# First batch group of a two-layer graph kernel: two columns of products become four tasks in two bank sets

## The chip, the cores and the metric

The kernel runs on one core of a Trainium2 chip. The metric is the device time of one execution in microseconds (us), lower is better. Three runs of the kernel before took 2121.89, 2118.05 and 2122.76 us; the median is 2121.89 us. A difference of about 0.2% (4.2 us) is what a measurement of this kernel can tell from no change.

## The reference

128 batches, each with 128 nodes and 512 features, go through two layers. All data is float32.

```python
# layer 0
deg = jnp.sum(adj, axis=-1, keepdims=True)
agg = jnp.einsum('bij,bjf->bif', adj, x) / jnp.maximum(deg, EPS)
cat = jnp.concatenate([x, agg], axis=2)
x   = _layernorm(x + jax.nn.relu(jnp.einsum('bnf,of->bno', cat, W)))
# layer 1
Xw = X @ Wv + bv
sj = Xw @ aw[:d, 0]
si = Xw @ aw[d:, 0]
e = leaky_relu(sj[:, None, :] + si[:, :, None] + ab[0], negative_slope=0.2)
alpha_matrix = A * jnp.exp(e)
transition = alpha_matrix / (jnp.sum(alpha_matrix, axis=-1, keepdims=True) + 1e-12)
for k in range(3):
    H = H + Xk @ Wk[k] + bk[k]
    Xk = jnp.einsum('bij,bjd->bid', transition, Xk)
x = _layernorm(x + relu(H))
```

Only two parts of it matter for this change. The first is the product of x with the two halves of W, for the first four batches. The second is the folding of constants: the kernel never forms Xw, but folds Wv and aw into two extra weight columns, and bv, ab and bk into constants that layer 1 uses.

## The kernel before

The 128 batches are worked in 32 groups of four. Layer 0 runs over all groups first, then layer 1. Within a group, x is split into an upper pair of batches (`xu`) and a lower pair (`xl`), and every large product is a fast block product with seven multiplications in place of eight (the constants `LEFT` and `RIGHT` name the seven left and right operands). The left operands need four sums of quarter blocks of x (`left_sums`, called by `x_inner`), after x has been loaded in blocks (`load_left`) and transposed on VectorE (`x_turn`). The right operands need four sums of quarter blocks of the weights (`w_inner(0)` for the two weight blocks of output column 0, `w_inner(1)` for those of column 1).

From the second group on, the scheme of seven is used a second time, over the blocks of batches and weights: the tasks `P12`, `P56`, `P74` and `T` of a group. It needs further sums, `w_outer(1)` to `w_outer(4)`, of 1792 columns each, two of them on VectorE and two on GpSimd. The first group can't wait for these sums, so the function `first` computes it with the inner scheme only. It computes output column 0 and then column 1, each as seven products, and each product covers both pairs of batches: four matmuls of 256 columns, `xu` into the left half of a PSUM bank and `xl` into the right half. Four banks (`bA`) hold the running sums, called X, Y, W and Z. The results of column 0 go to SBUF, to be multiplied by the normalized adjacency; those of column 1 are copied into the other four banks (`bB`), onto which `first_last` then accumulates that product.

A float32 matmul shows in the trace as two passes. A product of `first` therefore shows as eight passes, four on `xu` and four on `xl`.

The order of the work on each engine is written out by hand. `steps` is a list of pieces of tasks (one `yield` is one piece, mostly one product). Work beside the products is placed by a number: position 2t is just after piece t's own instructions, and 2t + 1 is after the pending evictions (`late`). `START` holds these positions for the beginning of the kernel. Inside an engine instructions keep this order, so an instruction that waits holds up all that stand behind it. Ahead of the list stand the first loads, which are put on two queues (SyncE's, shown as SP, and ScalarE's, shown as ACT), and the first transposes and sums. The load DMAs share eight completion semaphores in turn, so at most eight of them are on their way at a time.

`fold_constants` is a generator of seven pieces. It loads nothing itself; its matmuls use `bk_sb`, `aw_sb` and `wvt_sb`, and at its end it fills two banks once with zero-padded copies of the identity, to leave them in a defined state. In the kernel before its pieces stand between the products of the first group, and its matmuls use banks of `bB`.

Of the kernel before, what the change touches and what calls it, by code (L numbers as in the profile page):

```python
# [16 lines left out]
def kernel(  # L17
# [92 lines left out]
    wvt_sb = [p2.tile([P, 2, F], FP, name=f"wvt{i}", tag="y") for i in range(2)]  # L110
# [3 lines left out]
    bk_sb = p1.tile([K, F], FP, name="bk_sb", tag="TT")  # L114
# [5 lines left out]
    load_w0([nc.scalar], 1)  # L120
    load_w0([nc.scalar], 3)
    load_adj(0)
    for i in range(2):
        nc.sync.dma_start(wvt_sb[i], wvt[i * FH : (i + 1) * FH, :].rearrange("(c p) f -> p c f", p=P))
# [32 lines left out]
    def fold_constants():  # L157
        ones_row = ones[:].to_broadcast([P, P])
        pb, pc, pw = bB[0], bB[3], bB[0]
        nc.tensor.matmul(pb, ones_row[:K], bk_sb, start=True, stop=True)  # L160
        L_.copy(beta[:, 0, 254:], pb[:, :131])
        L_.copy(beta[:, 1, :381], pb[:, 131:])
        t4 = small.tile([P, NC], FP, name="t4")
        V.tensor_add(t4, aw_sb[:, 0], aw_sb[:, 1])
        V.tensor_mul(t4, t4, bv_sb)
        t1 = small.tile([P, 1], FP, name="t1")
        V.tensor_reduce(t1, t4, AX.X, ALU.add)
        yield
        nc.tensor.matmul(pc[:, :1], ones_row, t1, start=True, stop=True)
        V.tensor_sub(beta[:, 1], beta[:, 1], beta[:, 0])  # L170
        V.tensor_add(cc, pc[:, :1], ab_sb)
        yield
        for c in range(NC):
            nc.tensor.matmul(pw[:2], aw_sb[:, :, c], wvt_sb[c // 2][:, c % 2, :], start=(c == 0), stop=(c == NC - 1))
            if c % 2:
                yield
        w2row = p1.tile([2, NC, Q, R], FP, name="w2row", tag="TT")
        L_.copy(w2row, pw[:2].rearrange("t (q c s) -> t c q s", q=Q, c=NC))
        yield
        for c in range(NC):  # L180
            mm(pc[:, 2 * c : 2 * c + 2], w2row[:, c].rearrange("t q s -> t (q s)"), ident[:2, :2], c == 0)
        L_.copy(stage[:, :, 3 * F : 3 * F + 2], pc[:, : 2 * NC].rearrange("p (c t) -> p c t", c=NC))
        for t in (pw, pc):
            nc.tensor.matmul(t, ident, ident[:, None, :].to_broadcast([P, Q, P]), start=True, stop=True)
        yield
# [71 lines left out]
    def x_inner(n, p):  # L257
        need(("x_turn", n, p, 1))
        t = (xu, xl)[p][n]
        left_sums([S_, S_, S_, S_], [t[:, :, i] for i in range(7)])  # L260
# [71 lines left out]
    def p12(lane, g):  # L332
        r, c11 = rs[g], c11s[g] = blocks(p2, "r"), blocks(p2, "c11")
# [15 lines left out]
    def p74(lane, g):  # L349
        r, c22, c21 = rs[g], blocks(p2, "c22"), blocks(p2, "c21")  # L350
# [76 lines left out]
    def first(lane, g):  # L427
        c11, c21 = blocks(p2, "c11"), blocks(p2, "c21")
        c11s[g], c21s[g] = c11, c21

        def column(o, bank_of, evict):
            X, Y, W, Z = [bA[i] for i in bank_of]

            def prod(dst, k, start=False):
                for h in range(2):
                    for i in range(2):
                        mm(dst[:, h * FH : (h + 1) * FH], (xu, xl)[h][g][:, i, LEFT[k]], wf[:, SLOT[2 * i + o], RIGHT[k]],
                           start and i == h == 0)
            s5 = halves()
            prod(X, 1, True)  # L440
            L_.copy(Y, X)
            yield
            prod(Z, 5, True)
            L_.copy(s5, Z)
            yield
            prod(X, 6)
            V.tensor_add(W, X, s5)
            yield
            prod(Y, 2)
            yield  # L450
            prod(X, 7)
            evict(BY, Y)
            V.tensor_add(Z, X, s5)
            yield
            prod(W, 3)
            yield
            prod(X, 4)
            evict(BWW, W)
            evict(BZ, Z)
            late.append((evict, BX, X))  # L460
            yield

        def evict0(b, t):
            L_.copy(part(c11, b), t[:, :FH])
            V.tensor_copy(part(c21, b), t[:, FH:])
        yield from column(0, (0, 1, 2, 3), evict0)

        def evict1(b, t):
            i, h = b
            L_.copy(bB[i][:, h * FH : (h + 1) * FH], t[:, :FH])  # L470
            V.tensor_copy(bB[2 + i][:, h * FH : (h + 1) * FH], t[:, FH:])
        yield from column(1, (1, 2, 0, 3), evict1)
        lane[:] = [bA[2], bA[3], bA[1], bA[0]]

    def first_last(lane, g):
        new_mv(g)
        for p, t in ((1, c21s[g]), (0, c11s[g])):
            for i in range(2):
                b = 2 * p + i
                mm(bB[b], aTs[g][:, b], t[:, i, :, :FH])  # L480
                late.append((residual, g, b, bB[b]))
            yield
        lane[:] = [bB[2], bB[0], bB[1], bB[3]]
# [274 lines left out]
    TASKS = {"F": first, "FL": first_last, "P12": p12, "P56": p56, "P74": p74, "T": last, "O1": o1, "O2": o2, "O5": o5,  # L758
             "O6": o6, "O7": o7, "O4": o4, "O3": o3, "C": combine}
    lanes = [list(bA), list(bB)]  # L760
# [4 lines left out]

    PA = "p74.5 P12.1 P12.2 p74.6 P12.3 p74.7 P12.4 t.1 P12.5 P12.6 t.2 P12.7 P56.1 t.3 P56.2 t.4 t.5 P56.3 t.6 t.7 t.8 t.9 t.10 t.11 P74.1 P74.2 P56.4 P56.5 P56.6 P74.3 P56.7 P74.4".split()
# [7 lines left out]
    for k in range(14):  # L774
        step(0, "F", 0, k + 1)
# [84 lines left out]
    def fold(i):  # L860
        next(folding, None)
# [9 lines left out]
    def w_outer(i):  # L871
        need(("w_inner", 1), *{1: [], 2: [("w_outer", 1)], 3: [("F", 0, 14)], 4: [("w_outer", 2)]}[i])
# [4 lines left out]
        ("w_inner", 1): 9, ("x_s2", 1): 30, ("fold", 2): 3, ("a_turn", 0): 16, ("w_outer", 2): 16, ("fold", 4): 11,  # L877
        ("degree", 0): 10, ("a_norm", 0): 10, ("load_left", 1, 1): 9, ("x_s1", 1): 21, ("fold", 5): 16, ("fold", 3): 8,
        ("w_outer", 1): 11, ("fold", 7): 10, ("fold", 6): 17, ("x_s3", 1): 22, ("w_outer", 4): 19, ("load_y", 0, 0): 17,
        ("load_y", 0, 1): 9, ("x_turn", 1, 0, 0): 14, ("a_load", 0): 15, ("x_turn", 1, 0, 1): 14, ("x_inner", 1, 0): 16,  # L880
        ("x_turn", 1, 1, 1): 18, ("load_left", 1, 0): 12, ("x_turn", 1, 1, 0): 10, ("fold", 1): 4, ("x_inner", 1, 1): 19,
        ("w_outer", 3): 33, ("load_left", 2, 1): 19, ("load_adj", 1): 26, ("load_left", 2, 0): 23, ("load_wk",): 58,
    }
    OPS.update({f.__name__: f for f in (w_inner, w_outer, fold, load_wk)})
# [21 lines left out]
    for p in range(2):  # L906
        run([(x_turn, 0, p, 0), (x_turn, 0, p, 1)])
    run([(x_inner, 0, 0), (x_inner, 0, 1), (w_inner, 0)])
    gens, count, held_by = {}, {}, {}
    ET = mybir.EngineType  # L910
    with tc.manual_schedule(engines={ET.PE, ET.DVE, ET.Activation, ET.Pool, ET.SP}):
        for t, (lane, name, g, k) in enumerate(steps):
            if name:
                if (name, g) not in gens:
                    if lane in held_by:
                        need((*held_by[lane], {"F": 14, "FL": 2, "T": 11, "C": 8}.get(held_by[lane][0], 7)))
                    held_by[lane] = name, g
                    gens[name, g] = TASKS[name](lanes[lane], g)
# [33 lines left out]
```

## Time and profile before

| quantity | value |
|---|---|
| median of three runs | 2121.89 us (2118.05 to 2122.76) |
| the profiled execution's own time | 2123.95 us |
| its span, first to last instruction | 2122.2 us |
| TensorE busy | 2088.1 us, 98% of the span |
| VectorE, ScalarE, GpSimd busy | 69%, 54%, 73% of the span |
| first product of the first group starts | 11.06 us |
| first product of the second group starts | 51.32 us |

The profiled execution takes 1.75 us more than its span, and 2.06 us more than the median of the three runs. Times inside it are counted from the start of the span. A row of the timeline gives the start, the duration, the engine, the source line, the operation and its tiles, and the number of instructions that were merged into it; a note in square brackets tells how long the engine was idle before and what ended that. A row of a table of windows gives, for each stretch of time, the busy time of every engine with its number of instructions, the mean clock that TensorE was granted (1.00 is full speed), the share of the DMA engines that was in use, and what they moved.

### The profile page before, as it was taken

To read this page: it belongs to the slowest core of one execution; us is meant where nothing else is said; L and a number is where in the kernel's file an instruction comes from. 1 tells how busy PE (TensorE), PEld (TensorE's weight loads), DVE (VectorE), ACT (ScalarE), POOL (GpSimd) and SP (SyncE) were. 2 spreads that over 40 slices of the span, in tenths; PEclk is the share of its full clock that TensorE was granted. 3 is DMA by queue.
4 is the path that set the end of the run, shared out by engine and by line. 5 is a ranking of instruction groups with operands and counts; after the bars stand their busy time and mean duration, and the time that the engine had idled before them with its cause. 6 is when DMAs were issued, how large, how long until landed. Compare 5 with 4: busy or idle time off the path is not lost. (4 is left out here: it accounts for less than half of the span.)

```text
span 2122.2 us, 25957 instructions
## 1 busy us (share of the span) xinstructions
PE 2088.1 (98%) x7104; PEld 1329.5 (63%) x7104; DVE 1462.4 (69%) x3229; ACT 1149.4 (54%) x2885; POOL 1539.5 (73%) x1427
## 2 busy tenths in 40 slices
PE   8999999999999999999999999999999999999996
PEld 5887888888788886555555555555555555555552
DVE  4777777777777776666666666666666666666654
ACT  2665666666566665354454454554554554554554
POOL 4877888887777775767767777777677677677662
PEclk9999999999999999999999999999999999999998
DMA  7766666566666668235335335335335345344332
GB/s 170 181 192 188 188 185 175 159 187 193 162 174 181 181 170 236 68 96 131 92 101 130 89 100 137 82 100 139 80 102 134 84 106 132 82 111 128 83 86 95
DMA packets 429454, 287.13 MB, mean 135 GB/s; under 512 B 153465, under 2 KB 352249, under 8 KB 429308
## 3 DMA queue, kind: packets, MB, share of 16 engines
q1 hardware_dynamic: 428060, 283.62, 50.0%
q10 hardware_dynamic: 1120, 1.84, 0.4%
q8 instruction: 56, 0.92, 0.2%
q14 instruction: 90, 0.74, 0.1%
q0 software_dynamic: 128, 0.01, 0.0%
HBM read 191.60 MB, written 93.79 MB: 134 GB/s over the span
## 5 line engine op out<-in xcount | busy, mean ns | idle before, releaser
L149 PE MATMUL bA<-big,xu 128*128 128x256 f32 (+1 forms) x1834 | 579.9, 436 | 3.3 <-DVE r L611 1.0
L149 PEld LDWEIGHTS bA<-big,xu 128*128 128x128 f32 x1834 | 346.3, 190 | 178.5 <-issue 27.3
L149 PE MATMUL bB<-big,xl 128*128 128x256 f32 (+1 forms) x1330 | 398.9, 416 | 0.3 <-ACT bB L565 0.2
L149 PE MATMUL bA<-big,xs 128*128 128x256 f32 (+1 forms) x1316 | 387.9, 418 | 0.4 <-ACT bA L565 0.2
L149 PEld LDWEIGHTS bB<-big,xl 128*128 128x128 f32 x1330 | 251.7, 189 | 99.9 <-issue 14.8
L149 PEld LDWEIGHTS bA<-big,xs 128*128 128x128 f32 x1316 | 244.8, 189 | 93.0 <-DVE bA L574 14.6
L149 PE MATMUL bB<-big,xu 128*128 128x256 f32 (+1 forms) x868 | 286.5, 441 | 2.5 <-DVE bB L388 2.5
L149 PE MATMUL bB<-c,TT 128*128 128x512 f32 x512 | 247.6, 596 | 0.0
L608 POOL TENSOR_TENSOR s<-s,r 128x385 f32<-128x385 f32 x128 | 127.9, 1000 | 153.3 <-DVE bA L574 108.4
L493 ACT ACTIVATE junk<-y,mv 128x512 bf16<-128x512 f32 x256 | 184.5, 721 | 80.2 <-POOL mv L488 76.1
L149 PEld LDWEIGHTS bB<-big,xu 128*128 128x128 f32 x868 | 159.0, 189 | 91.8 <-DVE r L598 19.2
L506 ACT ACTIVATE y<-y,mv,rstd 128x512 f32<-128x512 f32 x256 | 204.1, 811 | 3.1 <-POOL mv L501 3.1
L149 PE MATMUL bA<-big,xl 128*128 128x385 f32 (+1 forms) x490 | 182.1, 478 | 4.6 <-DVE xl L254 4.5
L574 DVE TENSOR_TENSOR bA<-bA,s 128x385 f32<-128x385 f32 x128 | 72.5, 567 | 164.5 <-ACT s L571 117.8
L371 DVE SCALAR_TENSOR_TENSOR y<-bB,y 128x512 f32<-128x512 f32 x256 | 170.6, 683 | 19.8 <-PE bB L149 13.6
L149 PE MATMUL bB<-big,xs 128*128 128x385 f32 x448 | 173.4, 492 | 0.9 <-POOL xl L242 0.9
L149 PEld LDWEIGHTS bB<-c,TT 128*128 128x128 f32 x512 | 97.6, 191 | 90.4 <-issue 48.7
L745 ACT COPY bB<-r 128x512 f32<-128x512 f32 x64 | 37.7, 590 | 191.0 <-DVE big L744 189.3
L277 POOL TENSOR_TENSOR xu<-xu,xs 128x896 f32<-128x896 f32 x63 | 131.4, 2086 | 10.1 <-PE bA L149 10.1
L149 PEld LDWEIGHTS bA<-big,xl 128*128 128x128 f32 x490 | 93.8, 192 | 71.6 <-DVE c L611 7.9
L273 POOL TENSOR_TENSOR xl<-xu,xl 128x896 f32<-128x896 f32 x63 | 133.4, 2117 | 1.1
L269 POOL TENSOR_TENSOR xs<-xs,xu 128x896 f32<-128x896 f32 x63 | 131.8, 2092 | 2.4
(160 smaller groups left out, 3537.0 us busy)
## 6 DMA issues: line engine op xcount, KB each, us to landing
xb<-in_x_dram SPq DMA_DIRECT2D x256, 128.0 KB, 3.5
y<-in_x_dram SPq DMA_DIRECT2D x64, 512.0 KB, 4.4
yd<-y SPq DMA_DIRECT2D x64, 512.0 KB, 2.8
xb<-yd SPq DMA_DIRECT2D x256, 128.0 KB, 3.8
y<-yd SPq DMA_DIRECT2D x64, 512.0 KB, 4.3
out_dram<-y SPq DMA_DIRECT2D x64, 512.0 KB, 2.8
ag<-in_adj_dram SPq DMA_DIRECT2D x64, 256.0 KB, 3.9
sb<-sd SPq DMA_DIRECT2D x252, 64.0 KB, 3.2
```

The costliest lines, as they stand in the source:

```text
L149: nc.tensor.matmul(dst, lhsT, rhs, start=start, stop=True, skip_group_check=True)
L269: S_.tensor_sub(xs[n][:, 1], xs[n][:, 0], xu[n][:, 0])
L273: S_.tensor_sub(xl[n][:, 0], xu[n][:, 0], xl[n][:, 0])
L277: S_.tensor_sub(xu[n][:, 1], xu[n][:, 1], xs[n][:, 1])
L371: V.scalar_tensor_tensor(y, t, 0.0, y, ALU.max, ALU.add, accum_out=mvs[n][:, b, 0:1])
L493: L_.activation(junk, ys[n, b // 2][:, b % 2], AF.Square, bias=mvs[n][:, b, 0:1], accum_out=mvs[n][:, b, 1:2])
L506: L_.activation(y, y, AF.Identity, bias=mvs[n][:, b, 0:1], scale=rstds[n][:, b : b + 1])
L574: V.tensor_add(W, X, s5)
L608: S_.tensor_add(s5, s5, part(src, BZ, BW))
L745: L_.copy(at_[b], row(b, 254, 766, 1))
```

## The change

The change touches only the first group and what stands beside it and the second group.

1. `first` becomes four tasks: A is column 0 with the upper pair, B column 0 with the lower pair, C column 1 with the upper pair, D column 1 with the lower pair. Each has seven products of two matmuls. A and B share the banks `bA`, C and D the banks `bB`; A and C use the left halves of the banks, B and D the right halves. The list `PF` gives the order of the 28 pieces. Column 1 is now evicted into `bA`, and `first_last` and the second group's lanes have the bank sets exchanged.
2. The fold's seven pieces move from beside the first group to beside the second (after `first_last`), on two banks of `bA`. The load of `wvt` moves with them, to a place behind the store of the normalized adjacency.
3. Of the loads of weight blocks 1 and 3, half go from ScalarE's queue to SyncE's. SyncE's queue has the x blocks of the second group in another order, and the two loads of y (x in row order, for the residual) earlier.
4. The left sums of the first group go from GpSimd to VectorE; those of the lower pair, and its transposes, stand between the products of A and B. `w_outer(2)` and `w_outer(4)` stand ahead of the second group's left sums on GpSimd.

```diff
-    wvt_sb = [p2.tile([P, 2, F], FP, name=f"wvt{i}", tag="y") for i in range(2)]
+    wvt_sb = [p2.tile([P, 2, F], FP, name=f"wvt{i}", tag="c22") for i in range(2)]
...
     load_left(0, 1)
-    load_w0([nc.scalar], 1)
-    load_w0([nc.scalar], 3)
+    load_w0([nc.scalar, nc.sync], 1)
+    load_w0([nc.scalar, nc.sync], 3)
     load_adj(0)
-    for i in range(2):
-        nc.sync.dma_start(wvt_sb[i], wvt[i * FH : (i + 1) * FH, :].rearrange("(c p) f -> p c f", p=P))
+
+    def load_wvt():
+        for i in range(2):
+            nc.sync.dma_start(wvt_sb[i], wvt[i * FH : (i + 1) * FH, :].rearrange("(c p) f -> p c f", p=P))
...
     def fold_constants():
-        pb, pc, pw = bB[0], bB[3], bB[0]
+        need(("FL", 0, 2))
+        pb, pc, pw = bA[2], bA[3], bA[2]
...
-        left_sums([S_, S_, S_, S_], [t[:, :, i] for i in range(7)])
+        left_sums([S_ if n else V] * 4, [t[:, :, i] for i in range(7)])
...
+    def first(g, o, h):
+        X, Y, W, Z = [t[:, h * FH : (h + 1) * FH] for t in (bA, bB)[o]]
+        if o == 0:
+            dst = blocks(p2, "c21" if h else "c11")
+            (c21s if h else c11s)[g] = dst
+        else:
+            need(("w_inner", 1))
+
+        def prod(dst, k, start=False):
+            for i in range(2):
+                mm(dst, (xu, xl)[h][g][:, i, LEFT[k]], wf[:, SLOT[2 * i + o], RIGHT[k]], start and i == h == 0)
+
+        def evict(b, t):
+            if o == 0:
+                to = part(dst, b)
+            else:
+                need(("FA", 0, 7), ("FB", 0, 7))
+                to = bA[2 * h + b[0]][:, b[1] * FH : (b[1] + 1) * FH]
+            if (b[0] + b[1]) % 2:
+                L_.copy(to, t)
+            else:
+                V.tensor_copy(to, t)
+        s5 = halves()[:, :FH]
+        if h:
+            need(("F" + "AC"[o], 0, 2))
+        prod(X, 1, True)
+        L_.copy(Y, X)
+        yield
+        prod(Z, 5, True)
+        L_.copy(s5, Z)
+        yield
+        prod(X, 6)
+        V.tensor_add(W, X, s5)
+        yield
+        prod(Y, 2)
+        late.append((evict, BY, Y))
+        yield
+        prod(X, 7)
+        V.tensor_add(Z, X, s5)
+        yield
+        prod(W, 3)
+        late.append((evict, BWW, W))
+        yield
+        prod(X, 4)
+        late.append((evict, BZ, Z))
+        late.append((evict, BX, X))
+        yield
...
-    lanes = [list(bA), list(bB)]
+    lanes = [[bB[1], bB[3], bB[0], bB[2]], list(bA)]
...
+    PF = "A.1 A.2 A.3 A.4 A.5 A.6 B.1 B.2 B.3 C.1 B.4 A.7 C.2 B.5 C.3 B.6 B.7 C.4 C.5 C.6 D.1 D.2 D.3 D.4 D.5 D.6 C.7 D.7".split()
...
     START = {
...
+        ("fold", 2): 81, ("x_inner", 0, 1): 13, ("load_y", 0, 0): 7, ("fold", 5): 86, ("fold", 4): 85, ("degree", 0): 23,
+        ("load_left", 2, 1): 59, ("x_s3", 1): 50, ("w_outer", 3): 64, ("load_left", 2, 0): 36, ("x_turn", 1, 1, 0): 37,
+        ("x_turn", 1, 0, 1): 39, ("load_left", 1, 1): 17, ("load_y", 0, 1): 13, ("w_inner", 1): 16, ("load_wk",): 74,
+        ("fold", 3): 81, ("x_s2", 1): 54, ("a_norm", 0): 25, ("x_turn", 1, 0, 0): 30, ("fold", 6): 91, ("x_s1", 1): 48,
+        ("w_outer", 1): 22, ("w_outer", 2): 34, ("w_outer", 4): 37, ("load_wvt",): 32, ("fold", 7): 102,
+        ("x_inner", 1, 0): 44, ("a_load", 0): 35, ("x_turn", 0, 1, 1): 8, ("a_turn", 0): 59, ("x_turn", 1, 1, 1): 37,
+        ("load_left", 1, 0): 4, ("fold", 1): 77, ("x_inner", 1, 1): 38, ("load_adj", 1): 47, ("x_turn", 0, 1, 0): 6,
     }
...
-    for p in range(2):
-        run([(x_turn, 0, p, 0), (x_turn, 0, p, 1)])
-    run([(x_inner, 0, 0), (x_inner, 0, 1), (w_inner, 0)])
+    run([(x_turn, 0, 0, 0), (x_turn, 0, 0, 1), (x_inner, 0, 0), (w_inner, 0)])
```

## The prediction

> **What bounds the kernel now.** I read the page first, then the granted clock and busy time by stage, then the timeline of the first stages, then the waits of the start.
>
> ```profile
> PE 2088.1 (98%) x7104; PEld 1329.5 (63%) x7104; DVE 1462.4 (69%) x3229; ACT 1149.4 (54%) x2885; POOL 1539.5 (73%) x1427
> ...
> PE   8999999999999999999999999999999999999996
> ...
> PEclk9999999999999999999999999999999999999998
> ```
>
> TensorE is busy 98% of the span, and the slices show it full everywhere but in the first and last of 40. So the change can win only where TensorE isn't full, or runs slowly: at the start, which is all it touches.
>
> ```profile
> core 0: us, PE busy (x) PEld busy (x) DVE busy (x) ACT busy (x) POOL busy (x), PEclk, DMA share, GB/s
> 2.65:11.06 8.41, 8.41 (x16) 3.75 (x17) 1.73 (x5) 0.00 (x0) 3.05 (x8) 1.00 1.15 214
> 11.06:16.61 5.55, 1.03 (x5) 0.57 (x4) 4.55 (x7) 0.48 (x1) 2.55 (x3) 0.93 1.15 214
> 16.61:23.37 6.76, 6.76 (x14) 4.37 (x15) 0.54 (x1) 1.96 (x3) 2.85 (x4) 0.55 1.10 276
> 23.37:51.32 27.95, 27.95 (x119) 20.56 (x119) 14.10 (x25) 7.59 (x25) 13.82 (x11) 1.00 0.52 131
> 51.32:76.20 24.88, 24.88 (x107) 19.96 (x106) 19.59 (x40) 15.21 (x39) 21.56 (x19) 1.00 0.85 193
> ```
>
> The first stage is warming up on the identity. In the second TensorE has 1.03 us of work in 5.55. In the third it is busy, but at a granted clock of 0.55. The fourth is the rest of the first group, the fifth the second group with nothing missing: what a stage costs when it is fed.
>
> ```profile
> 11.06 1.03 PE L149 MATMUL bA<-big,xu 128*128 128x256 f32 x4
> ...
> 15.84 1.30 DVE L254 STREAM_TRANSPOSE xl<-xb 128x512 f32<-128x512 f32 x2 [1.00 <-issue]
> 16.13 1.28 ACT L441 ACT_TABLE_LOAD   x1 [16.13 <-DMA big<-in_w0t_dram]
> ...
> 16.61 2.07 PE L149 MATMUL bA<-big,xl 128*128 128x256 f32 x4 [4.52 <-DVE xl L254]
> ...
> 18.48 1.91 PE L149 MATMUL bA<-big,xu 128*128 128x256 f32 x4
> ...
> 24.34 1.03 PE L149 MATMUL bA<-big,xl 128*128 128x256 f32 x4
> ```
>
> ```profile
> PE bA L149 <- DVE xl L254: 4.5, 1, 4.5
> ```
>
> The first product does its four passes on `xu` at 11.06 us and stops: its four on `xl` need the transposes at 15.84, and those the last quarter of `xb`. TensorE stands from 11.93 to 16.61. Then four passes take 1.91 us (the next start 1.70 later) where the row at 24.34 takes 1.03 (the next 0.86 later): half speed, after the long wait. ScalarE issues loads until 16.1 and only then loads its table.
>
> **The ledger of the first group.** From 11.06 to 51.32 are 40.26 us. The eight block products are 112 passes of 0.2157 us (0.863 for four): 24.15. The fold lies among them: the bk matmul 1.34, the column of ones 0.14, the two pairs on `wvt` 1.90 each, the eight small ones and two identity fills 2.89, and 0.1 us more on the first pass behind each and before: 8.7. The rest, 7.4, is loss: the wait 4.7 with 0.4 of slow first pass, and eleven half-speed passes at 0.21 extra, 2.3.
>
> **Part 1, four tasks.** TensorE's work is the same 28 x 0.863. The order of pieces puts A.1 to A.6, all on `xu`, where the wait was. I walk through it with this trace's durations and the order and waits of the built program (not run). VectorE turns `xu` until 9.79 as now; then its four sums of 256 columns, at about 0.37 each (an estimate: a little over half of the 0.68 that 512 columns take in the row at 14.16), until 11.27; then `w_inner(0)` at 0.68 each until 14.0 (the first three took 1.1 to 1.2 now, beside GpSimd's sums, which took 1.05 to 1.17 then and 0.72 alone). A.1 starts at 11.06. A.2 needs the first weight sum, 11.95, and starts 0.08 late. A.3 to A.6 need sums of 12.6 to 14.0, ScalarE's copy of A.1 (12.2 to 12.5) and one addition on VectorE (14.4): all in time, A.6 ends at 16.30. The `xl` load keeps its place among the first twenty DMAs, so I leave the transposes at 15.84. On VectorE now stand: first transpose 16.50, an eviction (0.42) 16.92, an addition for A (0.43) 17.35, second transpose 18.0, first sum 18.37.
>
> [...] No row of this trace shows two tasks in the halves of one bank in this stage. [...] B.1 waits for A's addition, though that reads the other half. [...] B.2 needs the sum of 18.37 anyway. [...] Gaps so far: 0.08 + 1.10 + 0.16.
>
> B.2, B.3, C.1, B.4, A.7, C.2, B.5, C.3, B.6 follow from 18.42 to 26.15. VectorE meanwhile: addition for B.3 20.82, `w_inner(1)` 4 x 0.68 to 23.54, eviction 23.97, `w_outer(1)` 1.98 (the row at 33.22 now) 25.95, eviction 26.37, degree 0.34, and only then the addition that B.7 waits for, 27.18. B.7 starts 1.08 late. What is queued behind it there, the addition for C.3 (C.5 waits) and a transpose, is in time. With D.7's 0.65 the gaps make 3.07, and the group ends at 11.06 + 24.15 + 3.07 = 38.3. Twice as many evictions, copies and additions at 0.37 to 0.43 instead of 0.58 to 0.70 cost ScalarE about 0.7 and VectorE 0.6 us: off the path but where named.
>
> **The clock.** Windows show 1.00 until 11.06 and 0.55 after a wait of 4.7. With gaps of 1.1 at most I take the clock to stay: 2.3 + 0.4 won. [...]
>
> **Part 2, the fold.** Its matmuls go where TensorE is full, so its time is added there: 8.7 less 0.4 for the bk matmul, which fell into the slow clock (1.34, at full speed two passes of 0.43 and 0.1), so 8.3. Its waits: beta's two copies on ScalarE (0.76) have P12.7 and P56.1 before the next fold matmul; the copy of `w2row` (0.57) has one product of 0.86, as now. Without that cover, up to 0.8 each. `wvt` is loaded at about 33, used at 49.
>
> **Part 3, the loads.** Weight blocks 1 and 3 now need 24 DMAs of 128 KB in all ahead of `ag` and without `wvt`'s 1 MB: 3.1 MB at the 214 GB/s of the windows from about 2.5 us on, so by about 18, wanted by C.1 at 20.1 and VectorE at 20.8. If they came only at 22.1 as now, 1.3 lost. ScalarE has ten issues instead of fourteen and is free at about 10.6 rather than 16.1, which A.3 needs: with the old queue A.3 would stand until 18. SyncE has four more issues, then the second group's x blocks and 1 MB of y in front of its lower half: 0.26 + 0.5 + 1.05 + 0.5 MB at that rate, about 29; VectorE turns it at 30.5, and until 31.5 nothing waits. Then the adjacency's store (28), `wvt`, and the loads back, by about 36 (store to turn takes 33.98 to 41.33 now); the turn is wanted at 41. The wk loads (12 DMAs) stand six pieces nearer to the second group's start and hold SyncE's queue for some 13 us as now, ahead of the same store and loads; the folded wk is not wanted before the third group.
>
> **Part 4, GpSimd.** It starts at 26 with its two `w_outer`, 3.98 each, then two times four sums (0.75 with spacing): P12.2 needs 37.8 and comes at 39.1, P12.3 39.2 and comes at 40. Then three sums of 2.1, one slowed by VectorE's `w_outer(3)` as now (3.75): 47.8, wanted at 49. Slack about 1 us; each us later costs one.
>
> **The sum.** Loss 7.4 becomes 3.07, the fold is 0.4 cheaper: 4.7 us won. The profiled execution's 2123.95 (span 2122.2 and 1.75 around it, unchanged) becomes 2119.2; the median of the runs is 2.06 lower, so 2121.89 becomes 2117.2.
>
> **The rivals.** (a) Fewer gaps: if `xl` lands a little earlier, since `ag` and `wvt` no longer compete, or the small sums are shorter, and B.7's wait shrinks, 1.5 to 2.5 us less gap: gain 6 to 7.4, about 2115. Against it: the order on VectorE is fixed. Chance 0.17. (b) VectorE's queue or the clock eats it: `w_inner(1)` waits for late weights (1.3), GpSimd's sums come 1 us late[...]: gain 1 to 3, about 2120. For it: slacks near 1 us. Chance 0.20. (c) The change doesn't do what it says: A stalls on ScalarE's table load or copies and the wait only moves. Then the clock halves as well, gain near 0: 2121.9. Against it: ScalarE's wait is for the DMA slots alone. Chance 0.05. (d) Slower: the transpose of the second group's lower half stands on VectorE ahead of the addition for D.3, and its load stands behind y on SyncE. It is covered until it lands at 31.5; each us after that is lost to D.5, and to P12.2 through GpSimd. It has eaten the gain at 36.2, and is slower by over 0.2% (4.2 us) from 40.4 on: 2126.7 at 41. Against it: y's 512 KB land in 4.4 us in the median. Chance 0.04. My forecast: 0.54, its own range 2116 to 2118 (gain 3.9 to 5.9).
>
> **How the numbers follow.** 0.2% is 4.2 us, about what a measurement of this kernel can tell from no change. Of the forecast's gains of 3.9 to 5.9 five sixths lie above it: 0.45 faster, 0.09 same. With (a), faster is 0.62; same is 0.09 with (b) and (c), 0.34; slower is (d), 0.04. The range holds the forecast, nearly all of (a) and most of (b): 2114 to 2120.5. It is no narrower because the three runs alone lie 4.7 us apart.
>
> **What would show it.** Right: `xu` passes without a hole from 11.06 to 16.3, the clock 1.00 in all of it, gaps near 17, 18, 26 and 37, P12.1 at 38.3, the fold's matmuls between 47 and 60 with 8.3 us. Wrong: a clock under 1.00 after 11 us; a hole before A.3; P12.2 or P56.1 waiting for GpSimd; TensorE waiting beside the fold. If the second group starts at 38 and the time is not lower, it was lost later, and the forecast's step for the fold is wrong.

## The result, and the profile after

The changed kernel takes 2117.36 us in the median of 20 runs (2116.79 to 2118.60), the kernel before 2121.45 us in 20 runs beside it (2118.05 to 2124.02). The ratio is 0.9982, with a 95% interval of 0.9975 to 0.9989: 4.1 us or 0.18% won, where 4.7 us and 2117.2 were forecast. The forecast of a gain above 0.2% (chance 0.62) is missed by a little; the 0.18% is clear of no change all the same, since the interval ends at 0.11%. The runs also lie closer together, within 1.8 us instead of 6.0. The profiled execution of the changed kernel took 2118.59 us (span 2116.8), that of the kernel before 2123.95 (span 2122.2).

From the page of the changed kernel, the line of busy time and two rows of its slices:

```profile
PE 2086.5 (99%) x7104; PEld 1328.0 (63%) x7104; DVE 1464.2 (69%) x3241; ACT 1149.3 (54%) x2889; POOL 1531.9 (72%) x1419
...
PE   9999999999999999999999999999999999999996
...
PEclk9999999999999999999999999999999999999998
```

The first slice of TensorE is now a 9 as well; the last is the one that isn't full. Busy time and granted clock by stage, in the same columns as before: warm-up, the run on `xu`, the rest of the first group, the second group with the fold:

```profile
2.65:11.87 9.22, 9.22 (x17) 3.99 (x18) 2.71 (x6) 0.98 (x1) 1.94 (x6) 1.00 1.10 216
11.87:17.17 5.30, 5.30 (x25) 4.20 (x23) 4.55 (x10) 1.03 (x3) 0.00 (x0) 1.00 1.13 235
17.17:37.73 20.56, 19.83 (x90) 16.41 (x90) 14.93 (x30) 7.22 (x25) 11.78 (x8) 1.00 0.92 208
37.73:70.83 33.10, 33.10 (x132) 22.75 (x131) 20.54 (x44) 16.62 (x44) 24.30 (x23) 1.00 0.88 175
```

The stage that had 1.03 us of work in 5.55 has 5.30 in 5.30, and the clock column shows 1.00 in all four. In the first row it says too much: until 7.21 us the passes there start 0.85 us or more apart, behind it 0.43, so the first part of the warm-up still runs at half speed. The rows behind it, from the timeline and the groups by line (start, duration, engine, line, operation, and in brackets the idle time ahead of it with its releaser):

```profile
11.87 5.45 PE L151 MATMUL bA<-big,xu 128*128 128x256 f32 x24
15.75 0.71 DVE L257 STREAM_TRANSPOSE xl<-xb 128x512 f32<-128x512 f32 x1 [0.49 <-DMA xb<-in_x_dram]
17.17 3.05 PE L151 MATMUL bA<-big,xl 128*128 128x256 f32 x12
...
26.55 1.13 PE L151 MATMUL bA<-big,xl 128*128 128x256 f32 x4 [0.28 <-DVE bA L473]
...
36.76 1.13 PE L151 MATMUL bB<-big,xl 128*128 128x256 f32 x4 [0.45 <-ACT bA L454]
```

A.1 to A.6 run without a hole from 11.87 to 17.17; then B.1 follows at once. Two waits of note remain (0.2 us more are lost around B.2). The row of B.7 shows 0.28 us idle; counted from the start of one pass to the start of the next, 0.44 us are lost, and 0.10 more since the first pass behind a wait takes longer, 0.55 in all. For D.7 the row shows 0.45, and 0.72 are lost. The second group's first product starts at 37.73 us instead of 51.32. Of these 13.59 us the fold takes 8.07 back among the second group.

There is one more place that the prediction did not look at, and it explains part of the spread of the times. Between the two layers TensorE waits for VectorE, in both kernels alike. In the trace of the changed kernel:

```profile
815.71 0.81 PE L151 MATMUL bA<-big,xu 128*128 128x256 f32 x2 [2.48 <-DVE bA L395]
816.32 4.38 PE L151 MATMUL bB<-big,xu 128*128 128x385 f32 x8
```

and in a second trace of the same kernel (the run "after_again" below):

```profile
815.70 0.70 PE L151 MATMUL bA<-big,xu 128*128 128x256 f32 x2 [2.48 <-DVE bA L395]
816.24 3.04 PE L151 MATMUL bB<-big,xu 128*128 128x385 f32 x8
```

The wait of 2.48 us is the same and ends at the same time; behind it the same eight passes of 385 columns take 4.38 us in one execution and 3.04 in the other. In the first the clock was at 0.50 from 816.16 to 819.58, in the second at 1.00 (the rows stand in the last section). From this wait to the start of the last matmul the fourteen traces of this case take either 1283.2 to 1283.6 us or 1284.4 to 1285.2, whatever the kernel. The clock behind the wait is one thing in that difference: the second trace of the changed kernel, which kept it, has 1283.6, the first 1284.8. The clock is also at 0.50 once more near the end, from 2094.54 to 2101.37 in the trace before and from 2089.34 to 2096.16 in the first of the changed kernel, with the last matmul at 2105.91 and 2100.54. How the other short times divide between the two places was not shown. So the start of the pass behind this wait is the best measure of what a change in the first stages did. I call it the mark. Before it stood at 821.23, now at 815.71: 5.5 us.

### The profile page after: what moved, and what is told of

Same layout as the page of the kernel before. It is cut to its first block, busy times and chain, and to the rows that moved or that the text cites. A ratio compares the mean times of both kernels' runs of the same rounds, so it can differ in the third digit from the quotient of the medians.

```text
span 2116.8 us, 25969 instructions
## 1 busy us (share of the span) xinstructions
PE 2086.5 (99%) x7104; PEld 1328.0 (63%) x7104; DVE 1464.2 (69%) x3241; ACT 1149.3 (54%) x2889; POOL 1531.9 (72%) x1419
## 5 line engine op out<-in xcount | busy, mean ns | idle before, releaser
L151 PE MATMUL bB<-big,xu 128*128 128x385 f32 (+1 forms) x1806 | 571.5, 436 | 3.3 <-DVE r L620 1.0
L151 PEld LDWEIGHTS bB<-big,xu 128*128 128x128 f32 x1806 | 340.8, 190 | 174.4 <-issue 24.8
L151 PE MATMUL bA<-big,xl 128*128 128x256 f32 (+1 forms) x1358 | 406.3, 416 | 0.6 <-DVE bA L473 0.3
L151 PE MATMUL bB<-big,xs 128*128 128x256 f32 (+1 forms) x1316 | 388.5, 418 | 0.4 <-ACT bB L574 0.2
L151 PEld LDWEIGHTS bB<-big,xs 128*128 128x128 f32 x1316 | 244.8, 190 | 94.4 <-DVE bB L583 14.6
L151 PE MATMUL bA<-big,xu 128*128 128x256 f32 (+1 forms) x896 | 292.7, 439 | 2.6 <-DVE bA L395 2.5
L151 PE MATMUL bA<-c,TT 128*128 128x512 f32 x512 | 247.8, 597 | 0.0
L151 PEld LDWEIGHTS bA<-big,xu 128*128 128x128 f32 x896 | 164.1, 189 | 93.2 <-DVE r L607 19.3
L151 PE MATMUL bA<-big,xs 128*128 128x385 f32 x448 | 173.5, 492 | 0.9 <-POOL xl L245 0.9
L151 PE MATMUL bB<-big,xl 128*128 128x385 f32 (+1 forms) x462 | 172.3, 480 | 0.5 <-ACT bA L454 0.4
```

The costliest lines, as they stand in the source:

```text
L151: nc.tensor.matmul(dst, lhsT, rhs, start=start, stop=True, skip_group_check=True)
```

## The experiments

The theory: the gain is the long wait filled, and the half clock that followed it avoided, less small new waits; the fold was moved at its own price. The rivals: the gain lies in the order of the loads, in the sums on VectorE, in the fold, or the half clock has nothing to do with the wait. Each kernel was timed beside the kernel before. Both medians are in the text, then their ratio with its 95% interval; the marks are together in a table at the end.

### The clock alone: the wait filled with identity matmuls

```diff
 def prod(dst, k, start=False, fill=0):
     for h in range(2):
+        for t in (bB + bB)[:fill] if h else []:
+            nc.tensor.matmul(t, ident, ident[:, None, :].to_broadcast([P, Q, P]), start=True, stop=True)
         for i in range(2):
             mm(...)
...
-prod(X, 1, True)
+prod(X, 1, True, 0 if o else 8)
```

> The kernel before, with eight identity matmuls of 512 columns into the idle banks between the first product's passes on xu and those on xl: 3.4 us of work for TensorE inside the 4.7 us wait, nothing else moved. Theory (the wait costs its own length and then halves the clock): the wait stays, the passes behind 16.6 us take 0.216 us each, and the group ends 2.3 to 2.7 us earlier: 2118.8 to 2119.2 where before has 2121.45. Rival (the half-speed stretch comes with the time since the start, whatever TensorE did): granted clock near 0.55 from 16.6 to 23.4 as before, time unchanged. If the whole gain of the change were this clock, it would come out at 2117.4.

2122.33 us (2121.75 to 2123.48) against 2120.97; ratio 1.0007 (0.9999 to 1.0015). My filler was too long: a matmul on 512 columns of fp32 is two passes of 0.43 us, so eight took 6.87 us and not 3.4. The passes on `xl` started at 19.03 us, 2.4 later than before. Yet the window behind them shows full speed, and the mark stands 0.6 us earlier than in the trace before:

```profile
12.16:19.03 6.87, 6.87 (x18) 3.04 (x17) 4.06 (x5) 1.28 (x1) 3.98 (x5) 1.00 1.12 256
19.03:22.00 2.97, 2.97 (x14) 2.38 (x13) 0.00 (x0) 0.75 (x2) 1.01 (x2) 1.00 1.13 271
```

So the half-speed passes of that trace were worth 3.0 us (2.4 and 0.6), and they are gone with the wait. The second try has half as many, `0 if o else 4`:

> The kernel before with four identity matmuls in the first product's wait instead of eight: a matmul there is two passes of 0.43 us, so eight were 6.9 us and held up the passes on xl by 2.4; four are 3.4 us, end by 15.4 to 16.7, and hold nothing up. Theory (the clock halves because TensorE stands, and the half-speed stretch, of one or two windows of 3.4 us or none, is what spreads the times of the kernel before): the passes on xl start at 16.4 to 16.6 at full speed, 2119.9 (that of the eight less 2.4), and the runs lie within 1.5 us of each other. Rival (an idle remainder of 1.2 us is enough to slow the clock): median 2121, spread as wide as before.

2121.13 us (2119.67 to 2121.67) against 2121.38; ratio 1.0001 (0.9993 to 1.0010). Timeline and windows:

```profile
12.45 3.60 PE L437 MATMUL bB<-ident 128*128 128x512 f32 x8
16.50 1.13 PE L149 MATMUL bA<-big,xl 128*128 128x256 f32 x4 [0.46 <-DVE xl L254]
```

```profile
16.50:23.30 6.80, 6.80 (x29) 5.14 (x30) 1.40 (x3) 2.61 (x5) 2.86 (x4) 1.00 1.09 275
```

The passes on `xl` start at 16.50 at full speed, and the mark stands at 818.23, 3.0 us ahead of the trace before. The rival is refuted: with 3.43 us of identity passes in the wait and 0.46 left of it, the clock stands at 1.00 behind it, where the trace before has 0.55. But the forecast of the time (2119.9) failed: by the ratio nothing was won (0.2 us slower, interval from 1.5 faster to 2.1 slower). The trace of the kernel before was one with 6.83 us at half speed; by the times, its median run has less to win. Its runs fall into two clumps, four at 2119.7 to 2120.1 and nine at 2120.7 to 2121.7. Their medians lie 1.4 us apart; the clock halved or not behind the layers' wait made 1.34 (4.38 less 3.04) in the two traces above. More fell into the upper clump.

### The old order of pieces in the new kernel

```diff
-PF = "A.1 A.2 A.3 A.4 A.5 A.6 B.1 B.2 ...
+PF = "A.1 A.2 B.1 A.3 A.4 A.5 A.6 B.2 ...
-("x_turn", 0, 1, 1): 8, ... ("x_turn", 0, 1, 0): 6,
+("x_turn", 0, 1, 1): 3, ... ("x_turn", 0, 1, 0): 2,
```

> The changed kernel with B.1, the first piece on xl, third in the order (A.1 A.2 B.1 A.3 ...), and the two transposes of xl ahead of A.3's addition on VectorE: the same tasks, loads, sums and fold, but the hole is not filled. Theory: TensorE stands from about 13 us to 17.2, at which B.1 starts; 3.3 us are lost, and up to 2.7 more if a wait of 3.5 to 4.4 us halves the clock as the 4.7 us did: 2120.7 to 2123.4. Rival (the gain is in four smaller tasks, their loads or sums, not in the order of TensorE's pieces): 2117.4.

2121.52 us (2119.58 to 2124.53) against 2120.97; ratio 1.0004 (0.9996 to 1.0012). Timeline and windows:

```profile
16.38 2.04 PE L151 MATMUL bA<-big,xl 128*128 128x256 f32 x4 [3.08 <-DVE xl L257]
18.93 5.70 PE L151 MATMUL bA<-big,xu 128*128 128x256 f32 x16 [0.51 <-ACT bA L461]
```

```profile
13.10:16.38 3.28, 0.20 (x1) 0.03 (x1) 1.80 (x4) 0.37 (x1) 0.00 (x0) 0.96 1.09 222
16.38:22.93 6.55, 6.04 (x14) 4.34 (x14) 1.06 (x3) 0.36 (x1) 0.00 (x0) 0.50 1.15 275
```

B.1 waits 3.08 us for `xl`, a hole of 0.51 follows, and the clock is at 0.50 until 22.93. With the same tasks, loads, sums and fold, the whole gain is gone, and the spread of 5 us is back. Without the order on TensorE, and the two transposes that go with it on VectorE, nothing of the change is left.

### The loads: the old queue in the new kernel, the new queue in the old one

```diff
-load_w0([nc.scalar, nc.sync], 1)
-load_w0([nc.scalar, nc.sync], 3)
+load_w0([nc.scalar], 1)
+load_w0([nc.scalar], 3)
```

> The changed kernel with weight blocks 1 and 3 loaded by ScalarE alone, as before. Theory (ScalarE must be free by 13 us for the copy that A.3 needs): ScalarE issues loads until about 16.1 us and then loads its table, its copy of A.1 comes at 17.4 to 17.9, TensorE stands some 4.3 us behind A.2, B.1's small wait vanishes, and the clock may halve behind it: 3.3 to 6 us slower than the changed kernel, 2120.7 to 2123.4. Rival (the order of TensorE's pieces is all that matters): 2117.4, no hole behind A.2.

2122.83 us (2121.62 to 2125.28) against 2120.97; ratio 1.0007 (0.9999 to 1.0016). ScalarE's and TensorE's timelines, and the windows:

```profile
9.64 6.32 ACTq L106 DMA_DIRECT2D big<-in_w0t_dram  x6
15.99 1.28 ACT L461 ACT_TABLE_LOAD   x1 [15.99 <-DMA big<-in_w0t_dram]
17.29 0.36 ACT L461 COPY bA<-bA 128x256 f32<-128x256 f32 x1
```

```profile
17.70 6.77 PE L151 MATMUL bA<-big,xu 128*128 128x256 f32 x16 [4.12 <-ACT bA L461]
```

```profile
17.70:23.92 6.22, 6.22 (x15) 4.96 (x16) 2.17 (x5) 0.23 (x1) 0.00 (x0) 0.50 1.06 260
```

ScalarE issues until 15.99, loads its table, and copies A.1 at 17.29; A.3 stands 4.12 us for that copy and then runs at half speed. The order of pieces needs the two lines of loads: without them the wait only moves from `xl` to ScalarE. The converse, the same two lines in the kernel before:

> The kernel before with weight blocks 1 and 3 split over ScalarE's and SyncE's queues, as in the changed kernel; order, fold and sums as before. Theory: the wait for xl at 16.6 us and the half clock behind it stay, 2121.45 within 0.8. Rival (the gain came with the order of the loads): 2117 to 2119.

2119.92 us (2117.26 to 2121.29) against 2120.97; ratio 0.9993 (0.9985 to 1.0001). That is 1.5 us faster by the ratio, with an interval from 3.2 faster to 0.2 slower, and more than the 0.8 that I had allowed. So the times do not tell whether the two lines are worth something by themselves. Timeline and window:

```profile
16.37 1.99 PE L149 MATMUL bA<-big,xl 128*128 128x256 f32 x4 [3.95 <-DVE xl L254]
```

```profile
16.45:19.86 3.41, 3.41 (x8) 2.70 (x9) 0.46 (x1) 0.57 (x1) 2.71 (x4) 0.51 1.10 338
```

The wait (3.95 us by its row) and the half speed are still there. `xl` came 0.24 us earlier than in the trace before, and the half speed lasted 3.4 us (16.45 to 19.86) instead of 6.83, which is why its mark is 1.2 us earlier. One trace cannot say whether the shorter half speed is owed to the loads.

### The sums back on GpSimd

```diff
-left_sums([S_ if n else V] * 4, ...
+left_sums([S_] * 4, ...
```

> The changed kernel with the first group's eight sums of x back on GpSimd. Theory (they are in nobody's way on either engine): B.2 starts up to 0.4 us later, since a sum takes 0.73 us there and 0.43 on VectorE; VectorE is 3.5 us of work lighter, so B.7's wait of 0.44 goes; 2117.4 within 0.6. Rival (a good part of the gain is the sums on VectorE): 2118.5 or more, with a hole before A.2, A.3 or B.2 of over 1 us.

2118.70 us (2117.90 to 2120.12) against 2121.01; ratio 0.9990 (0.9982 to 0.9998), while the changed kernel in the same series has 2117.53. My theory fell here. TensorE's timeline:

```profile
18.76 1.13 PE L151 MATMUL bA<-big,xl 128*128 128x256 f32 x4 [0.21 <-POOL xl L245]
20.24 1.13 PE L151 MATMUL bA<-big,xl 128*128 128x256 f32 x4 [0.35 <-POOL xl L247]
...
27.70 1.13 PE L151 MATMUL bA<-big,xl 128*128 128x256 f32 x4 [0.28 <-DVE bA L473]
```

B.2 and B.3 each wait for GpSimd's sum, 0.38 and 0.52 us lost where the changed kernel loses 0.09 ahead of B.2 and nothing ahead of B.3, because four sums of 0.72 us follow each other more slowly than four of 0.42. And B.7's wait didn't go although VectorE had less to do: VectorE's chain to it begins with the addition for B.3, and what is taken off VectorE ahead of that shortens nothing. Some 0.8 us of the gain are the sums' (the mark is 1.2 later; the rest is B.1, 0.35 later since the first product started only at 12.34).

### The fold's matmuls doubled

```diff
-nc.tensor.matmul(pw[:2], aw_sb[:, :, c], wvt_sb[c // 2][:, c % 2, :], start=(c == 0), stop=(c == NC - 1))
+for t in (pc, pw):
+    nc.tensor.matmul(t[:2], aw_sb[:, :, c], wvt_sb[c // 2][:, c % 2, :], start=(c == 0), stop=(c == NC - 1))
```

> The changed kernel with each of the fold's four matmuls on wvt made twice, the extra one into the bank of the column of ones, where its sum is not used: four more matmuls of 0.86 us. Theory (TensorE is full beside the second group, so the fold costs there what it costs, and moving it won nothing): 3.4 to 3.6 us slower than the changed kernel, 2120.9 to 2121.1. Rival (the fold's matmuls fall into waits of the second group): 2117.5 to 2118.5.

2122.73 us (2121.94 to 2124.23) against 2121.38; ratio 1.0008 (1.0000 to 1.0016): 5.2 us above the changed kernel (2117.53 in another series), and 5.6 by the mark. Timeline of TensorE and of VectorE:

```profile
51.79 3.60 PE L178 MATMUL bA<-wvt,aw_sb 128*2 128x512 f32 x8 [1.78 <-DVE cc L174]
56.38 3.60 PE L178 MATMUL bA<-wvt,aw_sb 128*2 128x512 f32 x8
```

```profile
49.81 1.85 DVE L173 TENSOR_TENSOR beta<-beta 128x385 f32<-128x385 f32 x1
51.59 0.15 DVE L174 TENSOR_TENSOR cc<-bA,ab_sb 128x1 f32<-128x1 f32 x1
```

The four extra matmuls cost 3.43 us in full. The rest is a wait that I made: the first extra one writes the bank of the column of ones, which VectorE still had to read, and that stood behind a subtraction of 1.85 us; TensorE lost 2.0 there instead of 0.16. So the fold has its full price there, and its wait was 0.16 us where its next matmul goes to another bank than the one VectorE is reading, 2.0 where it doesn't.

### Again the changed kernel, and what its remaining waits are worth

> The changed kernel once more, beside the three that follow, for a second trace of it and as the measure for them: 2117.4 within 0.5. Theory: how many of the identity matmuls at the start run at half speed differs from run to run, so the first product starts anywhere from 11.0 to 11.9 us, but B.1 starts at 17.1 to 17.4 in any case, since xl sets it; no long wait and no half-speed pass after 11.9 us.

2117.53 us (2116.89 to 2118.71) against 2121.01; ratio 0.9984 (0.9977 to 0.9990). The first product started at 11.27 and B.1 at 17.12; the mark is 815.70, as in the first trace. Next, the two small degree operations behind the additions:

```diff
-("degree", 0): 23, ... ("a_norm", 0): 25,
+("degree", 0): 29, ... ("a_norm", 0): 30,
```

> The changed kernel with the two small degree operations (0.15 and 0.18 us on VectorE) and ScalarE's row sums behind the addition for C.3 instead of ahead of the addition that B.7 waits for, and the normalising one place later. Theory (B.7 waits for VectorE's queue, nothing else): its wait falls from 0.44 to about 0.1, 0.35 us won, 2117.0; nothing lost behind it, since the turned adjacency has 5 us to spare. Rival (B.7 waits for its bank or for the product): the same wait, 2117.4.

2117.59 us (2117.01 to 2118.98); ratio to the kernel before 0.9986 (0.9980 to 0.9993): no difference from the changed kernel, where 0.35 us were expected. VectorE's and TensorE's timelines:

```profile
24.91 0.42 DVE L456 COPY c<-bA 128x256 f32<-128x256 f32 x1
25.46 0.43 DVE L473 TENSOR_TENSOR bA<-bA,s 128x256 f32<-128x256 f32 x1
```

```profile
25.95 1.13 PE L151 MATMUL bA<-big,xl 128*128 128x256 f32 x4 [0.24 <-DVE bA L473]
```

Here the addition starts 0.13 us after the end of the copy ahead of it; with the degree operations between, it starts 0.20 after it (26.09 against 25.89). The loss ahead of B.7 fell from 0.44 to 0.40, and not to 0.1. Two operations with 0.33 us of busy time cost 0.07, since their starts overlap the ends of their neighbours.

Then, on top of that edit, P12.1 (the first product of the second group) ahead of D.7, with Z evicted a piece earlier:

```diff
+i = steps.index((5, "FD", 0, 7))
+steps[i : i + 3] = [steps[i + 2], steps[i], steps[i + 1]]
...
 late.append((evict, BWW, W))
+if o:
+    late.append((evict, BZ, Z))
```

> As the one before, and the second group's first product P12.1 ahead of D.7, with D's block Z evicted a piece earlier so that its bank is free for P12.1's copy. Theory (D.7 waits 0.61 us because ScalarE evicts another task's columns out of the same bank, and one product of 0.86 between them covers it): the wait goes, 2116.4 to 2116.6, and GpSimd's sums have 0.4 us to spare for P12.3. Rival (the wait only moves to P12.1, P12.2 or P12.3): 2117.0.

2118.14 us (2117.00 to 2119.11); ratio 0.9985 (0.9978 to 0.9991). D.7 no longer waits, but D.2 does. TensorE's timeline:

```profile
31.63 4.58 PE L151 MATMUL bB<-big,xl 128*128 128x256 f32 x20 [0.33 <-DVE bA L456]
...
37.78 1.03 PE L151 MATMUL bB<-big,xl 128*128 128x256 f32 x4
```

The early eviction was made for task C as well, and there it came to stand on VectorE behind two transposes; D.2 lost 0.49 us for that bank.

The last two start with six identity matmuls instead of eight, and have the degree operations where the changed kernel has them; the second also has P12.1 ahead of D.7, with the early eviction for task D alone:

```diff
-for t in bA + bB:
+for t in bA[:3] + bB[:3]:
     nc.tensor.matmul(t, ident, ...
```

> The changed kernel with six identity matmuls at the start instead of eight. Theory (with the wait filled, the start of the first product counts: where the warm-up runs at half speed for long, the eight end at up to 12.4 us and everything behind is late; six end at 9.5 to 11 us, ahead of xu's sums and of xl): the upper part of the changed kernel's times goes, 2117.1 with no run above 2117.8. Rival (the two clumps of its times have another cause, such as the landing of xl): median and spread unchanged, 2117.4 and 1.8 us. Second rival (less warm-up leaves the clock lower behind it): slower than 2118.

2118.08 us (2116.33 to 2120.32); ratio 0.9984 (0.9978 to 0.9991). The runs spread more and not less. The windows of its trace, cut at 3.41 us:

```profile
9.05:12.46 3.41, 1.85 (x6) 0.59 (x4) 3.31 (x7) 1.60 (x2) 0.00 (x0) 1.00 1.12 224
12.46:15.82 3.36, 3.18 (x8) 2.55 (x9) 2.02 (x4) 0.41 (x2) 0.00 (x0) 0.50 1.12 219
```

The first product starts at 9.73. Ahead of it TensorE waits for `xu`, and behind it for a weight block and a weight sum, for none of these over 1.1 us. In the first window TensorE is busy 1.85 us of 3.41. The second window runs at 0.50, though TensorE is fed in it. The start gained 2.1 us and the mark is 1.4 later. The two extra warm-up matmuls of the changed kernel cover these waits.

> The six identity matmuls, and P12.1 ahead of D.7, with the early eviction of block Z for task D alone (for task C it made a piece of D wait 0.49 us). The degree operations stand where the changed kernel has them. Theory: D.7's wait of 0.61 us goes and nothing takes its place, 2116.5. Rival (VectorE's or GpSimd's queue makes P12.2 or P12.3 wait for it): 2117.1.

2117.22 us (2116.53 to 2120.13); ratio 0.9982 (0.9976 to 0.9989). TensorE's timeline, and the window with its longest hole:

```profile
36.75 1.03 PE L151 MATMUL bB<-big,xl 128*128 128x256 f32 x4
37.62 2.59 PE L151 MATMUL bB<-big,xu 128*128 128x256 f32 x10
```

```profile
10.27:13.68 3.41, 2.55 (x12) 1.73 (x10) 3.34 (x7) 2.01 (x3) 0.00 (x0) 1.00 1.15 214
```

D.7's wait is gone and 0.16 us are lost behind it, ahead of a pass of P12.3. The start is the same as in the run before, yet the clock stayed at 1.00 here. In this execution the last five passes of the warm-up (0.43 us each) start at 7.83 us, where in the run before the last four start at 7.65, so the first product starts 0.25 us later and hardly waits for its weight block (0.12 us). One long hole is left (1.03 us) where the other had three (0.37, 0.81 and 1.06), and the window that holds it is busy for 2.55 us and not for 1.85. One trace of each doesn't say how often the start with six goes one way or the other. The mark is 815.27, 0.4 earlier than that of the changed kernel. In the times this is 0.1 to 0.3 us of the medians, less than they can tell: I have no version that beats the changed kernel measurably.

The marks (start of the pass behind the layers' wait, us), and from there to the start of the last matmul:

| kernel | mark | to the end |
|---|---|---|
| before | 821.23 | 1284.7 |
| changed | 815.71, again 815.70 | 1284.8, again 1283.6 |
| eight, four identity matmuls in the wait | 820.61, 818.23 | 1283.4, 1284.9 |
| old order of pieces | 822.06 | 1284.4 |
| old queue in the new, new queue in the old | 822.58, 820.01 | 1284.6, 1283.2 |
| sums on GpSimd | 816.88 | 1284.8 |
| fold doubled | 821.33 | 1284.9 |
| degree later; P12.1 ahead of D.7 | 815.15; 815.68 | 1284.6; 1283.3 |
| six at the start; with P12.1 ahead of D.7 | 817.07; 815.27 | 1285.2; 1285.1 |

The mark of the kernel with the degree later is no gain of its edit: `xl` landed 0.5 us earlier in that execution (first transpose at 15.19 instead of 15.70 and 15.75).

## Why the prediction was right, and where its sum was not

**The wait filled: right.** A.1 to A.6 stand where the wait was, without a hole. The experiments with the old order and the old queue show that both the order and ScalarE's early freedom are needed.

**The first product's start: not in the sum.** I took 11.06 us for fixed. It is not: of the sixteen passes of the eight identity matmuls three take 0.85 us or more in the trace before and five in the first of the changed kernel, where the others take 0.43, and the traces have starts from 11.06 to 12.37. In the changed kernel's first trace this cost 0.81 and swallowed the gap of 1.10 ahead of B.1. It cancels: late A.1, no gap; early A.1, a gap.

**The small gaps: too large.** Forecast 3.07; the trace has 1.70 and the late start, 2.5 together; the second trace, from 11.27, has 2.2 and 0.2. B.7 lost 0.44 and a slower first pass of 0.1, forecast 1.08: VectorE's chain from the end of B.3's addition to the end of B.7's took 5.7 us and not 6.4, since its operations overlap by up to 0.1 us each. D.7 lost 0.61 and 0.1, forecast 0.65 (0.24 lag and 0.37 copy, for ScalarE's eviction of C.7 out of D.7's bank), and the row at 36.76 names ScalarE's eviction as what D.7 waits for. It is a wait that the program sets; no run here shows what happens without it. A sum of 256 columns takes 0.42 to 0.43 us on VectorE, not the 0.37 that I estimated. Two ends in my walk are also added up a little short (A.6 at 16.32 and B.6 at 26.19 by its own figures), which changes nothing.

**The fold: right.** 8.3 forecast, 8.07 by the traces. The doubled fold shows that TensorE is full there: 3.43 us of matmuls cost 3.43. One wait I did not name: when the matmuls behind the column of ones also write the bank that VectorE still reads, 2.0 us are lost, more than the 0.8 that I gave as the limit of the waits I did name.

**Loads, GpSimd: right.** `xb`'s lower half landed at 26.8 (29 forecast), the adjacency's turn started at 36.0, `x_s2` was done at 47.56 (47.8 forecast), and P12.2 and P12.3 lost no more than 0.13 us. The sums on VectorE were costed at nothing, as a thing beside the path; they were worth some 0.8 us. The sum contained it unnoticed, since it walked through the new order.

**The clock: right in kind, wrong in size.** In the first trace of the changed kernel the clock is 1.00 from 7.21 to 816.16, and in the second A.1 to A.6 take 5.68 us against 5.45 and the rows of four passes behind them 1.03 as in the first. But the 2.7 us that I put on it are those of one execution with 6.83 us at half speed. The times say what is left in the median: with the clock kept and nothing else changed (four identity matmuls) the median is the same within -1.5 to +2.1 us. By the marks of that kernel and the changed one, 818.23 and 815.71, all of the change but the clock is worth 2.5. The lowest clump of the runs before (11 of 41 at 2119.1 to 2119.9, in the series with eight identity matmuls) lies 2.2 us above the lower 13 of the changed kernel's 20 (2116.8 to 2117.6), by their medians. What is left of the 4.1 is some 1.6 us for the clock in the average run; that is a difference of two figures, at the edge of what the times with four identity matmuls allow.

So that the sum 7.4 - 3.07 + 0.4 = 4.7 came so near 4.1 is partly luck: two terms are off in opposite directions. In the traces it is 7.4 - 1.70 - 0.81 + 0.63 = 5.5 (the last term is the fold, 8.7 less 8.07), and the median has about 1.1 to 1.4 us less of half speed to lose than that trace. Of the rivals, (a) was the nearest for the gaps; (b)'s half speed did not come in the changed kernel, but the kernel with six warm-up matmuls had it (0.50 from 12.46 to 15.82), with holes of 1.06 us at most. (c) is what the old queue does. (d) did not come: the load landed 4.7 us ahead of its point.

What stays open: how often the kernel before ran with none, 3.4 or 6.8 us of half speed in its first stages was not seen, since only profiled executions show passes. The mean granted clock of its runs goes with their times: of the 57 beside the kernel with six warm-up matmuls, those at 2119.37 to 2120.08 have 0.995 or 0.996, the six at 2123.98 to 2124.17 have 0.993. Open is also why the upper clump was nine of thirteen with four identity matmuls, and three of thirteen with eight.

## What to carry to other kernels

A wait at the start is best filled with work that needs only what has landed, and the engine that must hand over inside that work (here ScalarE's copy, for which A.3 stood 4.12 us with the old queue) has to be free by then, or the wait only moves. Price a half-speed stretch with the median of runs, not with one trace, and compare traces at a mark ahead of the next long wait, so that the clock behind that wait is not counted. Small holes are not free of the clock: here one wait of 2.48 us was followed by half speed in one trace of the changed kernel and not in the other, and three holes of 0.37, 0.81 and 1.06 us in 3.41 us were followed by it, where one of 1.03 was not. Before two tasks share a bank, ask who reads it between two products, and put another bank's product there: with P12.1 ahead of D.7, 0.61 us lost became 0.16.

## What the runs showed of the hardware

In the trace before and in the first trace of the changed kernel the changes of the granted clock lie whole multiples of 3.413 us apart. In the trace before TensorE's slow warm-up ends at 5.58 us, and the clock is at 0.50 from 15.82 to 22.65, from 821.37 to 824.78 and from 2094.54 to 2101.37: 3, 2, 234, 1, 372 and 2 times 3.413 us. In the first trace of the changed kernel the slow warm-up ends at 7.21, and the clock is at 0.50 from 816.16 to 819.58 and from 2089.34 to 2096.16: 237, 1, 372 and 2 times. In the first stages of other kernels the rows at 0.50 or 0.51 are 3.41 us long with the new queue in the old kernel (16.45 to 19.86), 3.36 with six warm-up matmuls (12.46 to 15.82), 6.55 with the old order and 6.22 with the old queue. The trace before, cut in such steps:

```profile
9.01:12.41 3.40, 3.08 (x10) 1.43 (x8) 2.56 (x7) 0.00 (x0) 2.45 (x3) 1.00 1.15 210
12.41:15.82 3.41, 0.00 (x0) 0.00 (x0) 2.43 (x3) 0.00 (x0) 1.20 (x2) 1.00 1.14 205
15.82:19.22 3.40, 2.61 (x6) 2.16 (x7) 1.30 (x2) 1.78 (x2) 1.91 (x3) 0.50 1.09 331
19.22:22.62 3.40, 3.40 (x8) 2.20 (x8) 0.00 (x0) 0.56 (x2) 0.94 (x2) 0.50 1.16 248
22.62:26.03 3.41, 3.41 (x15) 2.40 (x14) 0.56 (x1) 0.75 (x3) 0.00 (x0) 1.00 0.24 40
```

The window with nothing in it is followed by one at 0.50; that one still has the end of the wait in it (2.61 us busy), and one more at 0.50 follows, busy for all of its 3.40 us; the next is at 1.00.

Behind the wait of 2.48 us between the layers the two traces of the changed kernel differ. In the first the wait (813.23 to 815.71) ends 0.45 us ahead of a change of the clock and lies whole in the row ahead of it. In the second (813.22 to 815.70) no change follows, and in rows of the same length the wait is divided between two. First the first trace, then the second:

```profile
812.75:816.16 3.41, 0.93 (x5) 0.50 (x4) 2.04 (x5) 1.65 (x4) 3.24 (x2) 1.00 1.03 312
816.16:819.58 3.42, 3.42 (x8) 1.76 (x7) 1.31 (x3) 0.45 (x1) 0.67 (x1) 0.50 0.93 297
```

```profile
811.56:814.97 3.41, 1.66 (x8) 1.02 (x6) 2.24 (x6) 2.62 (x6) 3.23 (x3) 1.00 1.06 308
814.97:818.39 3.42, 2.67 (x8) 1.54 (x9) 1.90 (x5) 0.48 (x1) 1.85 (x1) 1.00 0.78 302
```

In the trace before it is as in the first: the wait ends at 821.23, and the clock is at 0.50 from 821.37 to 824.78. That the division of the wait kept the clock in the second trace is my reading of these three traces; it was not shown. One kernel, then, has executions with the clock halved behind this wait and executions without: the same eight passes took 4.38 and 3.04 us.

I had not expected how little idleness is enough. With six warm-up matmuls the row from 9.05 to 12.46, which has holes of 0.37, 0.81 and 1.06 us and 1.85 us of busy time, is followed by one at 0.50. With P12.1 ahead of D.7 as well, the row from 10.27 to 13.68 has one hole of 1.03 us and 2.55 us of busy time, and the clock stays at 1.00 up to 19.23. The busy column alone does not order the cases: the row from 811.56 to 814.97 above is busy for 1.66 us, less than 1.85, and the row behind it is at 1.00. That column counts a pass of 256 columns as 0.38 us, though in A.1 to A.6 most follow each other 0.216 us apart. How much idleness halves the clock was not shown.
